# Depthwise convolution in halves of 64 rows, spread over bands 10 to 32, and the projection to 256 over three regions

## Chip, cores and metric

The kernel runs on one core of one Trainium2 chip. The metric is device time in microseconds (us) of one execution; the number given for a kernel is the median of several runs. A run taken with the hardware profiler is a separate execution with its own time, and all durations of single instructions come from it.

The engines are called as in the profile: PE is the tensor engine (PEld its weight loads), ACT the scalar engine, DVE the vector engine, POOL the general engine, SP the engine that issues nearly all DMAs here, one after the other in program order.

## The reference

The kernel computes two layers on x of shape (4, 128, 128, 128): four images, 128 channels, 128 x 128 pixels, all in 32-bit floats. Cut to what matters:

```python
# layer 0
tok  = regions(x, size=16, step=14)              # 9 x 9 regions of 16 x 16 pixels, overlapping by 2
y    = ln(tok) @ w_qkv                           # q, k, v; 4 heads of 32
tok  = softmax(q @ k.T * 32**-0.5) @ v @ w_out + b_out + tok
xf   = average of the overlapping regions, back on the image
y    = ln(xf) @ w_p0 + b_p0                      # 128 -> 256 channels: "the projection to 256"
ym   = depthwise_conv(y, dw_k, 5 x 5, padding 2) # each of 256 channels by itself
ym   = batchnorm(ym)                             # statistics over all images and pixels
x    = gelu(gelu(ym)) @ w_p2 + b_p2 + xf
# layer 1
out  = batchnorm(conv3x3(act_quant(x), weight_quant(w1)))
out  = batchnorm(conv3x3(act_quant(out), weight_quant(w2))) + x
```

The depthwise convolution of an image can begin only as the rows of `y` that it reads are projected, and the GELU stage can begin only when the statistics of the convolution of all four images are there.

## The kernel before

**The bands.** The first stage goes over 36 bands, t = 0 to 35: four images of nine bands, a band being a row of nine regions (`NR` = 9). For each region j the program records one attention: `scores` (PE, then two exponentials of ACT, L792), `halves`, `values_in`, and `values` of the region before. Beside these, `beside(t)` hands out side work to the nine regions as four lists each (`plan`): the layer norm and the q, k projections of band t + 1 (`ln1_chunks`, pieces `a1`, `a2`), the output projection, layer norm and projection to 256 of band t - 1 (`post_chunks`, two chunks `b1` and `b2` of eleven pieces), and steps of the depthwise convolution (`c[j]`, and `d[j]` where a region gets two). The order of the instructions on PE, ACT, DVE and SP is the order in which the program records them (`manual_schedule`); no scheduler moves them. Each engine takes its instructions in that order.

**The projection to 256.** The last four pieces of each chunk, `b1[7:]` and `b2[7:]`, are `p0`: four matmuls of 512 or 384 columns into a PSUM tile `pm` (three buffers), an ACT copy with bias into `y` (L567), and a store of `y` to DRAM (`y2_d`, L431, DMA `y_d<-y`) that is issued by SP after the next piece. There are four `y` tiles, two for each half of the channels, so a fifth `p0` writes where the first one's store must have landed. From band 10 on, the four of `b1` stand in region 8 and the four of `b2` in region 0 of the next band (`left`, `f`). Up to band 9 they are spread over three regions (`full`).

**The depthwise convolution.** `conv_steps(n)` makes the steps of one unit `(b, g, ng)`: image b, `ng` groups of `GR` = 16 rows from group g. A step reads one tile `u` (80 partitions: two half-tiles of 40 rows; `32 * CW` numbers each), does the matmuls of `depthwise` (L601) with a banded weight `w`, has ACT copy two PSUM tiles to `c` (L648), DVE take statistics (L652) and SP store to `cv_d`. With ng = 8 a tile is 4 + 4 channels of eight row groups and a unit has 32 tiles; with ng = 4 it is 8 + 8 channels of four row groups and a unit has 16 tiles. The first step (`begin`) only loads. `load(at + 2)` is issued in step `at`; where a tile begins a new weight block it loads `w` too (L587), just ahead of its four loads of `u` (L634). Pool `up` holds three `u` and three `w`; `c` has two buffers for each of two names.

**When steps run.** `todo` holds the steps, `share[0]` the bands over which they are to be spread. Images 0 and 1 are units of 33 steps over nine bands each (bands 10 to 18 and 19 to 27: 3 or 4 steps a band), image 2 of 33 steps over five (bands 28 to 32: 6 or 7 a band). Image 3 is three units: 17 steps in bands 33 and 34, 17 in band 35, and the rest (`conv_rest`) behind the last band. Before band 10 `todo` holds the preparation of weights.

`st0` keeps the statistics of each unit; `chunk_stats` merges them in `conv_rest`.

Of the kernel before, what the change touches and what calls it, by code (L numbers as in the profile page):

```python
# [8 lines left out]
F32 = mybir.dt.float32  # L9
# [5 lines left out]
P = 128  # L15
# [4 lines left out]
NR = (P - RS) // STEP + 1  # L20
# [11 lines left out]
GR = 16  # L32
CW = P // 2
KD = 2 * (GR + 4)
NCK = 8
# [11 lines left out]
def layers(  # L47
# [29 lines left out]
    nc = tc.nc  # L77
    B = x.shape[0]
# [45 lines left out]
    g1, b1 = vector(ln1_g, "g1"), vector(ln1_b, "b1")  # L124
# [3 lines left out]
    g2, b2 = vector(ln2_g, "g2"), vector(ln2_b, "b2")  # L128
# [7 lines left out]
    with (  # L136
# [21 lines left out]
        for w in (wqkv, wp0.rearrange("p h m -> p (h m)")):  # L158
            n = w.shape[1]
# [7 lines left out]

    bands = [(b, i) for b in range(B) for i in range(NR)]

    units = [(b, 0, P // GR) for b in range(B - 1)] + [(B - 1, g, n) for g, n in ((0, 4), (4, 2), (6, 2))]  # L170

    sctx = ctx.enter_context(ExitStack())
    stp = sctx.enter_context(tc.tile_pool(name=f"st0_{tag}", bufs=1))
# [11 lines left out]
    with ExitStack() as actx:  # L185
        pool = lambda name, bufs, **k: actx.enter_context(
            tc.tile_pool(name=f"{name}_{tag}", bufs=bufs, **k)
        )
# [8 lines left out]
        bctx = actx.enter_context(ExitStack())  # L197
        pool = lambda name, bufs: bctx.enter_context(tc.tile_pool(name=f"{name}_{tag}", bufs=bufs))
        xp, yp, sums = pool("xp", 2), pool("yp", 2), pool("sums", 1)
        up, cp = pool("up", 3), pool("cp", 2)  # L200
        att, attn_t, attn_v = pool("att", 2 if safe else 4), pool("attn_t", 2), pool("attn_v", 2)


# [381 lines left out]
        def weights(wt, k, jj, n, dma):  # L585
            for half in range(2):
                dma(  # L587
                    out=wt[64 * half : 64 * half + KD].rearrange("p s c m -> p s (c m)"),
                    in_=dw_d[2 * k + half, :, :, 256 * jj : 256 * (jj + n)],
                )  # L590
# [24 lines left out]
        def conv_steps(n, ahead=2):  # L615


            b, g0, ng = units[n]
            nc_ = min(8, 32 // ng)
            tiles = [(k, jj, c) for k in range(NCK) for jj in range(2) for c in range(0, 8, nc_)]  # L620
            steps, U, W = [], {}, {}
            nj = nc_ // 4

            def load(at):
                k, jj, c = tiles[at]
                if c == 0:
                    W[k, jj] = up.tile([P, 3, 8, 32], F32, name="w")
                    weights(W[k, jj], k, jj, 1, nc.sync.dma_start)
                ut = up.tile([P, 32 * CW], F32, name="u")[:, : ng * nc_ * CW]
                U[at] = ut = ut.rearrange("p (g c x) -> p g c x", g=ng, c=nc_)  # L630
                for half in range(2):
                    ch = 32 * k + 16 * half + 8 * jj + c
                    for a, z in ((0, GR), (GR, GR + 4)):
                        nc.sync.dma_start(  # L634
                            out=ut[64 * half + 2 * a : 64 * half + 2 * z].rearrange(
                                "p g c x -> p g (c x)"
                            ),
                            in_=input_of(b, g0, ng, ch, nc_, a, z),
                        )

            def products(at):
                k, jj, c0 = tiles[at]
                ut, wt = U.pop(at), W[k, jj]
                pc = [ps_m.tile([P, nj, ng, CW], F32, name="pm") for _ in range(2)]
                depthwise(pc, wt[:, :, c0:], ut, nc_)
                for half in range(2):
                    cv = cp.tile([P, nj, ng, CW], F32, name=f"c{half}")
                    nc.scalar.copy(  # L648
                        cv.rearrange("p j g x -> p (j g x)"), pc[half].rearrange("p j g x -> p (j g x)")
                    )  # L650
                    for j in range(nj):
                        nc.vector.bn_stats(  # L652
                            st0[:, k, half, 2 * jj + c0 // 4 + j, n, :], cv[:, j].rearrange("p g x -> p (g x)")
                        )
                        ch = 32 * k + 16 * half + 8 * jj + c0 + 4 * j
                        store(
                            bass.AP(
                                cv_d[b].tensor,
                                cv_d[b][g0, ch, 0:1].offset,
                                [[CW, P], [2 * P * GR * P, ng], [1, CW]],  # L660
                            ),
                            cv[:, j],
                        )

            def begin():
                for at in range(ahead):
                    load(at)

            steps.append(begin)
            for at in range(len(tiles)):  # L670
                def one(at=at):
                    if at + ahead < len(tiles):
                        load(at + ahead)
                    products(at)

                steps.append(one)
            return steps

        def conv_rest(n, w_t, u_t, c_t):
# [3 lines left out]
            b, g0, ng = units[n]  # L683
            early = 3
            at = GR + 2
# [12 lines left out]
            W = [w_t.tile([P, 3, 16, 32], F32, name=f"w{k}") for k in range(NCK)]  # L698
# [13 lines left out]
            def step(k):  # L712
                sc = ps_s.tile([P, 2, 2, NT], F32, name=f"sc{k % 2}")
                pc = [
                    sc[:, half].rearrange("p a n -> p (a n)").rearrange("p (j g x) -> p j g x", j=4, g=ng)
                    for half in range(2)
                ]
                depthwise(pc, W[k], U[k], 16)
                for half in range(2):
                    cv = c_t.tile([P, 4, ng, CW], F32, name=f"c{half}")  # L720
                    nc.scalar.copy(
                        cv.rearrange("p j g x -> p (j g x)"), pc[half].rearrange("p j g x -> p (j g x)")
                    )
                    for j in range(4):
                        nc.vector.bn_stats(
                            st0[:, k, half, j, n, :], cv[:, j].rearrange("p g x -> p (g x)")
                        )
                    engine = (nc.sync, nc.scalar)[half]
                    for g in range(ng):
                        engine.dma_start(  # L730
                            out=bass.AP(
                                cv_d[b].tensor,
                                cv_d[b][g0 + g, 32 * k + 16 * half, 0:1].offset,
                                [[CW, P], [4 * GR * P, 4], [1, CW]],
                            ),
                            in_=cv[:, :, g],
                        )
# [143 lines left out]
        def beside(t, sel=None):  # L881
# [3 lines left out]
            one = list(early) if t else ln1_chunks(1)  # L885
            early[:] = ln1_chunks(t + 2) if t + 2 < T else []
            two = post_chunks(t - 1, sel) if t else []
            had = len(todo)
            if t >= 2:
                b, i = bands[t - 2]  # L890
                if i == NR - 1 and b < B - 1:
                    todo.extend(conv_steps(b))
                    share[0] = NR if b < B - 2 else 5
                elif b == B - 1 and i == 4:
                    todo.extend(conv_steps(B - 1))
                    share[0] = 2
                elif b == B - 1 and i == 6:
                    todo.extend(conv_steps(B))
                    share[0] = 1

            fresh = len(todo) > had
            n = len(todo) // share[0] if fresh else -(-len(todo) // max(share[0], 1))
            conv = [todo.pop(0) for _ in range(n)]
            share[0] -= 1
            a1, a2 = one if one else ([None] * 9,) * 2
            b1, b2 = two if two else ([None] * 11,) * 2
            if t == T:
# [5 lines left out]

            c = [[] for _ in range(NR)]
            d = [[] for _ in range(NR)]
            twice = len(conv) > NR
            for j in sorted((1, 3, 5, 7, 8, 4, 6, 2, 0)[: len(conv)]):
                c[j] = [conv.pop(0)]
                d[j] = [conv.pop(0)] if twice and j and conv else []
            x1 = lambda: fetch(t, 0)  # L920
            x2 = lambda: fetch(t, 1)
            f, left[:] = list(left), b2[7:]
            s1 = early[0][0] if early else None
            plan = [
                ([a1[1]], [], f, [*c[0], a1[2]]),
                ([], [a1[3], *c[1]], [], [a2[0]]),
                ([a2[1]], [a1[4]], b1[:2], [*c[2], a2[2]]),
                ([], [a2[3], *c[3]], [], [b1[2]]),
                ([b1[3]], [a2[4]], [*a1[5:], *b2[:2]], [*c[4], b1[4]]),
                ([], [b1[5], *c[5]], [], [b2[2]]),  # L930
                ([b2[3]], [b1[6]], a2[5:], [*c[6], b2[4]]),
                ([], [b2[5], x1, *c[7]], [], []),
                ([], [b2[6], x2], b1[7:], [*c[8], s1]),
            ]
            if t == 0:
                plan[0] = ([], [], [], [*c[0], *a1[:3]])
# [12 lines left out]
                    flush(n)  # L949

        T = len(bands)
        todo, share, left, early = [], [0], [], []
        wq, kscale = [], []
        one, two = quantised(0, w1), quantised(1, w2)
        for n in range(len(one) + 1):
            todo += one[n : n + 1] + two[max(n - 1, 0) : n]
        todo += band_matrices()
        share[0] = NR + 1
        for blk in row_blocks(0):
            xb[0, blk[0]] = load_rows(xp, "xt", 0, *blk)  # L960
        bng, bnb = vector(bn_g, "bng"), vector(bn_b, "bnb")
# [445 lines left out]
```

## Time and profile before

| what | us |
|---|---|
| median of 3 runs | 3232.88 (3232.2 to 3239.54) |
| the profiled execution | 3249.98 |
| its span, first to last instruction | 3248.2 |
| bands 0 to 9 (0 to 506.2, with what stands ahead of them) | 506.2 |
| bands 10 to 18 (506.2 to 1022.5) | 516.3 |
| bands 19 to 27 (1022.5 to 1540.2) | 517.7 |
| bands 28 to 32 (1540.2 to 1913.9) | 373.7 |
| bands 33 to 35 (1913.9 to 2195.5) | 281.6 |
| from there to the GELU stage (2322.4) | 126.9 |
| GELU and both 3x3 convolutions (2322.4 to the end) | 925.8 |
| PE busy in the whole span | 3059.6 (94%) |
| ACT, DVE, POOL busy | 1988.5, 2014.5, 840.9 |

A band begins with its first exponential (L792, 18 in a band); the times are read from the trace. In a row of the stretches that are shown below, the numbers are the stretch, its length, the busy time and the instructions of each engine, the granted PE clock as a share of full speed, and the mean busy share of 16 DMA engines with what they moved in GB/s. In a row of the order of time, they are start, length, engine, line, operation, the tiles and shapes, the number of merged instructions and, in brackets, the idle time of the engine ahead of them and what ended it. Every 32-bit matmul of the program stands as two records.

### The profile page before, as it was taken

How to read it: one execution, taken by the hardware profiler on the slowest of the kernel's cores; microseconds unless marked ns; L12 is line 12 of the kernel's file. 1: busy time of each engine (PE TensorE's matmuls, PEld its weight loads, DVE VectorE, ACT ScalarE, POOL GpSimd, SP SyncE). 2: the span in 40 equal slices, each digit the busy share in tenths (PEclk: the TensorE clock that was granted, in tenths of full speed). 3: DMA queues.
4: the chain of work that ended last, by engine and by line, in shares of the span. 5: the costliest groups of instructions: out<-in, count | busy, mean ns of one | idle time of the engine just before them, and what ended most of it. 6: DMA issues, size and time to landing. Idle time of an engine off the chain costs nothing.

```text
span 3248.2 us, 92154 instructions
## 1 busy us (share of the span) xinstructions
PE 3059.6 (94%) x39162; PEld 1480.1 (46%) x39162; DVE 2014.5 (62%) x3244; ACT 1988.5 (61%) x2658; POOL 840.9 (26%) x1058
## 2 busy tenths in 40 slices
PE   7999999999999999999888998876899999999998
PEld 4555544444444444444344444453544444444443
DVE  5777886766766777676555664542455555666543
ACT  5777777777776777677555655432477777433443
POOL 3444443333333333333222232211111111000000
PEclk9999999999999999999999998876799999999999
DMA  3555677888886888886898988857899999452398
GB/s 82 151 167 162 176 186 191 203 199 204 215 193 169 191 206 211 196 213 172 179 202 201 209 188 203 196 158 187 264 354 359 358 359 304 162 167 80 110 357 311
DMA packets 809891, 681.70 MB, mean 210 GB/s; under 512 B 580918, under 2 KB 695935, under 8 KB 809471
## 3 DMA queue, kind: packets, MB, share of 16 engines
q1 hardware_dynamic: 798879, 669.17, 75.8%
q8 instruction: 311, 5.10, 0.7%
q0 software_dynamic: 1024, 3.93, 0.5%
q10 hardware_dynamic: 9568, 2.61, 0.3%
q14 instruction: 109, 0.89, 0.1%
HBM read 408.72 MB, written 270.79 MB: 209 GB/s over the span
## 4 chain that ended last, share of the span: by engine, by line
PE 76%; DMA 9%; ACT 5%; issue 4%; SPq 3%; DVE 2%; ACTq 0%; POOL 0%; DVEq 0%; POOLq 0%
PE pc L1164 21%; PE pm L438 16%; PE sc L784 9%; PE pm L601 9%; PE po L847 8%; PE pb L1228 6%; PE po L855 3%; DMA y_d<-y 3%; PE pm L377 3%; ACT pt L792 2%; DMA u<-y_d 2%; DMA xn<-row 1%; SPq L451 1%; SPq L431 1%; ACT v L775 1%
## 5 line engine op out<-in xcount | busy, mean ns | idle before, releaser
L867 DVE RECIPROCAL rd<-po 128x256 f32<-128x256 f32 x324 | 568.8, 1756 | 439.1 <-PE po L855 438.5
L1164 PE MATMUL pc<-q,wq 128*128 128x512 fp8e4 x3168 | 700.3, 381 | 5.1 <-DVE q L1176 5.1
L792 ACT ACTIVATE pt<-sc 128x1024 f32<-128x1024 f32 x648 | 628.2, 1025 | 119.1 <-PE sc L784 63.2
L802 POOL TENSOR_TENSOR sm<-pt 128x512 f32<-128x512 f32 x324 | 415.7, 1283 | 1047.3 <-ACT pt L792 727.0
L1164 PEld LDWEIGHTS <-wq 128*128 128x128 fp8e4 x3168 | 309.0, 98 | 406.7 <-issue 38.9
L784 PE MATMUL sc<-q,kr 32*128 32x256 f32 x5184 | 413.6, 417 | 27.3 <-ACT pt L792 27.1
L601 PE MATMUL pm<-u,w 40*32 40x504 f32 (+5 forms) x7680 | 369.6, 503 | 41.7 <-DMA u<-y_d 29.7
L784 PEld LDWEIGHTS sc<-q,kr 32*128 32x128 f32 x5184 | 254.1, 191 | 286.4 <-issue 177.1
L847 PE MATMUL po<-pt,v 128*32 128x256 f32 x5184 | 364.9, 401 | 10.0 <-DVE part L871 6.9
L648 ACT COPY c<-pm 128x512 f32<-128x512 f32 (+1 forms) x256 | 132.4, 563 | 272.3 <-PE pm L601 243.3
L438 PE MATMUL pm<-xn,wp 128*32 128x512 f32 (+1 forms) x2304 | 248.1, 553 | 44.6 <-ACT y L567 42.6
L567 ACT ACTIVATE y<-pm,vectors 128x512 f32<-128x512 f32 (+1 forms) x288 | 183.1, 641 | 166.0 <-DMA y_d<-y 111.9
L802 DVE TENSOR_TENSOR sm<-pt 128x512 f32<-128x512 f32 x324 | 244.2, 754 | 35.8 <-ACT pt L792 35.8
L438 PE MATMUL pm<-xn,wqkv 128*32 128x512 f32 (+1 forms) x2304 | 245.3, 548 | 4.9 <-ACT v L775 3.5
L601 PEld LDWEIGHTS pm<-u,w 40*32 40x32 f32 x7680 | 147.6, 112 | 223.1 <-issue 153.0
L652 DVE BATCH_NORM_STATS2 st<-c 128x6 f32<-128x512 f32 (+2 forms) x320 | 160.9, 550 | 134.8 <-ACT c L648 134.3
L1228 PE MATMUL pb<-cv,wp 128*128 128x512 f32 x512 | 232.1, 596 | 4.9 <-ACT cv L1219 4.9
L847 PEld LDWEIGHTS po<-pt,v 128*32 128x32 f32 x5184 | 140.5, 112 | 186.5 <-issue 103.5
L1172 DVE BATCH_NORM_STATS2 st<-pc 128x6 f32<-128x512 f32 x256 | 165.7, 689 | 84.7 <-PE pc L1164 84.7
L855 PE MATMUL po<-sm,ones 128*32 128x256 f32 x2592 | 206.1, 389 | 0.0
L874 POOL TENSOR_TENSOR ob<-ob,part 128x32 f32<-128x32 f32 x288 | 127.2, 442 | 230.6 <-DVE part L871 224.8
L438 PE MATMUL pm<-wqkv,yr 128*32 128x128 f32 x5184 | 176.3, 273 | 1.2 <-issue 1.2
(157 smaller groups left out, 3394.2 us busy)
## 6 DMA issues: line engine op xcount, KB each, us to landing
cv<-cv_d SPq DMA_DIRECT2D x64, 1024.0 KB
u<-y_d SPq DMA_DIRECT2D x234, 256.0 KB
cv_d<-c SPq DMA_DIRECT2D x192, 256.0 KB
y_d<-y SPq DMA_DIRECT2D x160, 256.0 KB
xn<-row SPq DMA_DIRECT2D x76, 512.0 KB
xfl<-xf_d SPq DMA_DIRECT2D x64, 512.0 KB
id_d<-y SPq DMA_DIRECT2D x64, 512.0 KB
idt<-id_d SPq DMA_DIRECT2D x64, 512.0 KB
```

Of the source, the lines that this page charges most:

```text
L438: nc.tensor.matmul(out[m], w[:, m], v, start=True, stop=True)
L567: nc.scalar.activation(y[:, :n], pm[:, : n * P].rearrange("p (r c e) -> p r e c", r=n, e=2), AF.Identity, bias=bp0[:, h : h + 1],)
L601: nc.tensor.matmul(outs[half][32 * q : 32 * q + 32, j, :, a:z], wt[hs, s, c, :], ut[hs, :, c, a + s - 1 : z + s - 1], start=(s == 1), stop ...
L784: nc.tensor.matmul(sc[h // 2][:, h % 2, kc, :].rearrange("p (r c) -> p r c", c=RS), region(kr, j)[hs, kc * P : (kc + 1) * P], queries(j, h ...
L792: nc.scalar.activation(pt, sc[p], AF.Exp)
L802: add(sm, pt[:, :, 0, :], pt[:, :, 1, :], ALU.add)
L847: nc.tensor.matmul(po[hs, 0, :], v[:, kc, hs], pt[h // 2][:, h % 2, kc, :], start=(kc == 0), stop=(kc == 1),)
L855: nc.tensor.matmul(po[hs, 1, :], ones, sm[h // 2][:, h % 2, :], start=True, stop=True)
L867: nc.vector.reciprocal(rd, po[:, 1, :])
L1164: nc.tensor.matmul(pc[:, h], w[:, t, :], q1[b][:, r + dy : r + dy + RB, dx : dx + P], start=(t == 0), stop=(t == 8),)
L1172: nc.vector.bn_stats(st[:, 2 * n + h, :], pc[:, h])
L1228: nc.tensor.matmul(pb[:, m], wp2[:, h, :], cv[:, h, px], start=(h == 0), stop=(h == 1))
```

## The change

Four things change.

1. Images 0 to 2 are cut into two units of 64 rows each (ng = 4) instead of one of 128 (ng = 8). The steps per image go from 33 to 34; a step keeps its size, but has 48 matmuls of 256 columns where it had 24 of 512, four stores of 128 KB where it had two of 256 KB, and its own weight block where two steps shared one.
2. The 102 steps of images 0 to 2 are given out evenly over the bands 10 to 32 (`left_over`): five a band in bands 10 to 19, four in bands 20 to 32. A unit joins when its rows are there (`waiting`). Bands 33 to 35 keep their numbers of steps.
3. The weights of a step are loaded one step ahead (`load_weights(at + 1)`), into a pool `wp` of two buffers. `c` has one name with three buffers, in `conv_rest` too.
4. From band 10 to 31 the last two `p0` of `b1` move from region 8 to the next band: two in region 8, three in region 0, three in region 2 (`f[:3]`, `f[3:]`). Band 32 and later keep four and four.

```diff
-    units = [(b, 0, P // GR) for b in range(B - 1)] + [(B - 1, g, n) for g, n in ((0, 4), (4, 2), (6, 2))]
+    units = [(b, g, 4) for b in range(B - 1) for g in (0, 4)] + [(B - 1, g, n) for g, n in ((0, 4), (4, 2), (6, 2))]
...
-        up, cp = pool("up", 3), pool("cp", 2)
+        up, wp, cp = pool("up", 3), pool("wp", 2), pool("cp", 3)
...
+            def load_weights(at):
+                if at == len(tiles):
+                    return
+                k, jj, c = tiles[at]
+                if c == 0:
+                    W[k, jj] = wp.tile([P, 3, 8, 32], F32, name="w")
+                    weights(W[k, jj], k, jj, 1, nc.sync.dma_start)
+
             def load(at):
                 k, jj, c = tiles[at]
-                if c == 0:
-                    W[k, jj] = up.tile([P, 3, 8, 32], F32, name="w")
-                    weights(W[k, jj], k, jj, 1, nc.sync.dma_start)
...
-                    cv = cp.tile([P, nj, ng, CW], F32, name=f"c{half}")
+                    cv = cp.tile([P, nj, ng, CW], F32, name="c")
...
             def begin():
+                load_weights(0)
                 for at in range(ahead):
                     load(at)
...
                 def one(at=at):
+                    load_weights(at + 1)
                     if at + ahead < len(tiles):
                         load(at + ahead)
                     products(at)
...
-                    cv = c_t.tile([P, 4, ng, CW], F32, name=f"c{half}")
+                    cv = c_t.tile([P, 4, ng, CW], F32, name="c", bufs=3)
...
-                if i == NR - 1 and b < B - 1:
-                    todo.extend(conv_steps(b))
-                    share[0] = NR if b < B - 2 else 5
...
-            n = len(todo) // share[0] if fresh else -(-len(todo) // max(share[0], 1))
+                if i in ((4, 6) if b == B - 1 else (4, NR - 1)):
+                    waiting.append(conv_steps(2 * b + (i > 4)))
+            last = T - NR + 6
+            while t > NR and waiting:
+                todo.extend(waiting.pop(0))
+            if t <= NR:
+                n = -(-len(todo) // (NR + 1 - t))
+            elif t < last:
+                n = min(len(todo), -(-left_over[0] // (last - t)))
+                left_over[0] -= n
+            else:
+                n = len(todo) // 2 if t == last else len(todo)
...
-                d[j] = [conv.pop(0)] if twice and j and conv else []
+                d[j] = [conv.pop(0)] if j and len(conv) > NR - 1 - j else []
...
-            f, left[:] = list(left), b2[7:]
+            apart = t + 1 < last
+            f, left[:] = list(left), [*(b1[9:] if apart else []), *b2[7:]]
+            g = 3 if t < last else len(f)
...
-                ([a1[1]], [], f, [*c[0], a1[2]]),
+                ([a1[1]], [], f[:g], [*c[0], a1[2]]),
...
-                ([a2[1]], [a1[4]], b1[:2], [*c[2], a2[2]]),
+                ([a2[1]], [a1[4]], [*f[g:], *b1[:2]], [*c[2], a2[2]]),
...
-                ([], [b2[6], x2], b1[7:], [*c[8], s1]),
+                ([], [b2[6], x2], b1[7 : 9 if apart else None], [*c[8], s1]),
...
+        left_over = [2 * (B - 1) * (2 * NCK + 1)]
```

## The prediction

> **What bounds the kernel now.** I read the chain of work that ended last, to see which engine sets the time; then the busy time by stretches with a cut at every band; then the order of time on PE, ACT and SP where the slow bands lose theirs.
>
> ```profile
> PE 76%; DMA 9%; ACT 5%; issue 4%; SPq 3%; DVE 2%; ACTq 0%; POOL 0%; DVEq 0%; POOLq 0%
> ```
>
> PE sets the time, and DMA waits are next. The bands, by stretches (band 10; 19; 20; then 28 to 35):
>
> ```profile
> 506.20:566.00 59.80, 56.12 (x848) 26.90 (x840) 38.95 (x61) 41.35 (x62) 19.66 (x25) 0.97 0.84 193
> ...
> 1022.50:1082.70 60.20, 57.11 (x832) 27.14 (x824) 37.50 (x59) 40.30 (x60) 19.59 (x25) 0.94 0.82 183
> 1082.70:1138.80 56.10, 55.98 (x928) 26.56 (x923) 40.32 (x63) 41.48 (x65) 21.14 (x27) 1.00 0.84 189
> ...
> 1540.20:1608.60 68.40, 65.01 (x984) 29.71 (x976) 40.54 (x65) 43.47 (x67) 19.90 (x25) 0.95 0.80 173
> 1608.60:1688.00 79.40, 71.21 (x1072) 32.43 (x1068) 45.38 (x71) 44.74 (x71) 21.12 (x27) 0.94 0.92 201
> 1688.00:1763.30 75.30, 68.63 (x1072) 31.91 (x1068) 43.98 (x69) 44.61 (x70) 21.13 (x27) 0.95 0.90 205
> 1763.30:1843.10 79.80, 71.05 (x1072) 32.07 (x1068) 45.32 (x70) 44.71 (x70) 21.13 (x27) 0.94 0.89 202
> 1843.10:1913.90 70.80, 65.71 (x1024) 29.89 (x1020) 43.20 (x68) 43.59 (x68) 21.13 (x27) 0.95 0.89 201
> 1913.90:1996.50 82.60, 75.24 (x1397) 41.37 (x1390) 43.36 (x79) 44.92 (x70) 21.11 (x27) 0.90 0.83 192
> 1996.50:2094.80 98.30, 83.84 (x1592) 45.68 (x1591) 49.68 (x95) 46.19 (x73) 19.98 (x24) 0.86 0.83 198
> 2094.80:2195.50 100.70, 74.99 (x1908) 48.37 (x1909) 40.58 (x100) 35.23 (x62) 15.38 (x18) 0.78 0.63 167
> ```
>
> Band 20, with four products, is all PE at full clock. Bands 29 to 31, with seven, lose 4 to 9 us of idle PE and run at a clock of 0.94 to 0.95. What one product costs PE, with 512 columns and with 256:
>
> ```profile
> 655.66 2.78 PE L601 MATMUL pm<-u,w 40*32 40x512 f32 x48
> ...
> 1943.99 2.79 PE L601 MATMUL pm<-u,w 40*32 40x256 f32 x96
> ```
>
> So a band without products is 56.10 - 4 x 2.78 = 45.0 us, and band 29 should take 45.0 + 7 x 2.78 = 64.5; it takes 79.4. Its successor shows where that goes (first PE, then ACT, then SP, as band 30 begins):
>
> ```profile
> 1690.07 2.39 PE L438 MATMUL pm<-xn,wp 128*32 128x384 f32 x24
> 1696.94 0.98 PE L438 MATMUL pm<-xn,wp 128*32 128x384 f32 x8 [4.48 <-ACT y L567]
> ```
> ```profile
> 1696.30 0.58 ACT L567 ACTIVATE y<-pm,vectors 128x384 f32<-128x384 f32 x1 [5.40 <-DMA y_d<-y]
> ```
> ```profile
> 1688.14 3.49 SPq L451 DMA_DIRECT2D xr<-in_x_dram  x1
> 1691.72 3.56 SPq L431 DMA_DIRECT2D y_d<-y  x3
> ```
>
> The fifth `p0` needs the `y` tile of the first; that tile's store was issued some 9 us after the copy, because SP first had the loads and stores of the step in region 7 and a fetch of `xr`. ACT stands, the three `pm` fill, PE stands, and the clock is granted at half for 3.4 us at a time after it (eight such windows, two of them doubled, between 1608 and 1865). In bands 28 to 32 the excess over 45.0 + 2.78 per product is 9.5, 14.9, 10.8, 15.3 and 9.1 us: 60 together. Bands 10 and 19 (two products, floor 50.6) lose 9.2 and 9.6, to the same wait and to the first loads of an image, which must wait for its last `y`. The four-product bands 11 to 16 and 20 to 25 take 57.4 in the mean, 1.3 above 56.1.
>
> **The change, part by part.**
>
> *Halves of 64 rows.* PE: 96 products of 2.79 us instead of 96 of 2.78: 1 us. ACT: two copies of 128x512 a step as before. DVE: four statistics of 413 ns (the 128x256 row) for two of 684: 0.28 us a step, beside a DVE at 40 of 57 us; without that cover it would be 27 us. The Trainium skill ("TensorE: Matmul & The Clock Gate", on the 56 ns gap) speaks against small matmuls: about 62 ns each when the sequencer decodes them in software, by which 96 records would take 6 us and the change would cost some 300 us. The row above has 96 in 2.79, 29 ns each, so the measurement decides, and the sum goes by it.
>
> *More issues on SP.* A step issues four `u`, two `w`, four stores: 10, where it was seven on average. By medians (`u` 0.35, `w` 0.77, store 0.46 us) that is 4.8 us against 3.1. A five-step band has 18 + 50 = 68 issues: 24 us for the steps, 8 for the rest and the waits in the queue (SP now holds 30 to 34 us in a four-step band), some 45 of 60. It hides while SP is not the bound; that is the second rival. DMA time: shares of 0.85, 0.90 and 0.87 in bands 11 to 13 are 49.6 us of all engines in the mean, 0.92, 0.90 and 0.89 in bands 29 to 31 are 70.6, so 7.0 a step. The second weight block adds 120 packets of 1 KB at 79 ns over 16 engines, 0.6, and the longer `u` packets give back 0.2 (640 of 79 ns against 320 of 147, the means of the packet records by size). A five-step band then wants 58.6 us, a four-step band 51.2. The skill ("DMA: Bandwidth & Descriptors", how many engines) has a copy of 40 partitions run on ten engines only, so the weights would load those more than the mean shows; no trace here tells the engines apart.
>
> *Even spread and three regions.* Between a `p0` and the one that needs its tile there is as much PE work as before, but only one `p0` of region 0 now depends on a store of region 8, where four did, and PE has `scores` and `values` (1.15 + 1.68 us) to run while ACT stands. Four-step bands have no step in region 8 at all. I take the stall of a four-step band at 1.0 us (1.3 now; from 0.3 to 2). A five-step band shows nowhere: at least nothing over its floor (band 20 has that), 1 us as the low end; at most what a DMA share of 0.92, the highest in any band, allows: 58.6 / 0.92 = 63.7, 5.6 over the floor. I take 3, as the step in region 8 keeps part of the late store. First loads of an image no longer wait, since they read rows done bands ago.
>
> Bands 10 to 19: 10 x 45.0 + 47 products x 2.79 + 5 (two bands with 16 rows instead of 14, 2.3 to 2.7 each) = 586, + 30 = 616; before 576.5. Bands 20 to 32: 13 x 45.0 + 49 x 2.79 + 5 = 727, + 13 = 740; before 831.2. Together 1356 against 1407.7: **52 saved**.
>
> *Weights one step ahead, three `c`.* In bands 10 to 32 steps lie 11 to 19 us apart, and a weight issued where SP now loads `u` would land with 2 us or more to spare; only region 7 to 8 (9 us) is tight. In bands 33 to 35 it isn't spare: putting each weight where the next step's was issued, with 2.3 us to land (as their packets show there), 21 of 28 steps find it 0.2 to 7.0 us late, 65 us added up. SP is behind PE there, so a stall that PE pays lets SP catch up, and the next is smaller. Low end 2 us gained (the first step of a unit waits for one weight less), high end 35, half of it paid; I take 12. A copy of ACT into the third `c` waits for the store of the step before instead of two before; 16 of 32 would come 1 to 8 us before that store is even issued, hidden partly by the same stalls: 2 more. The longer merge of statistics (54 numbers for 36) adds 0.7 behind the last step. **14 to 15 lost.**
>
> Sum: 1356 - 1407.7 + 14 = -38 on a span of 3248.2: 3210. The profiled execution lies 17 above the median, so 3232.9 - 38 = **3195 us**.
>
> **The rivals.**
>
> *Late weights take it all back (slower, 0.14).* If lag isn't caught up, bands 33 to 35 pay the 65 us, and region 8 of each five-step band pays what the nearest rows of band 28 lack (3.5 us late) with half a clock window of 3.4, 5.2 x 10 = 52: 3195 + 51 + 52 = 3298. It turns slower when 38 us of that is paid, a third. For it: those bands already stand at a clock of 0.78 to 0.90. Against: own slack of weights there is 1 to 16 us now, and each stall slows the copies that SP waits for.
>
> *SP or DMA bounds the five-step bands (0.14).* At 0.92 they take 63.7, or about 5.6 over the floor: 3195 + 26 = 3221. For it: shares of 0.92 in band 29. Against: band 34 passes 107 issues in 98.3 us, 0.92 each, and 68 at that are 62.6.
>
> *The waits vanish wholly (0.12).* 1 and 0.3 of stall, nothing in the tail: 587 + 9 + 727 + 4 = 1327, 81 saved: 3152.
>
> That the steps don't land as said is excluded: the built order has the matmuls of five and four steps in those bands and `p0` as 3, 3 and 2.
>
> **How the numbers follow.** The forecast has 0.60. Runs spread by 0.23%, so 0.3% (9.7 us) is told from nothing. Faster takes most of the forecast (0.57), the third rival (0.12) and some of the second (0.05): 0.74. Same is the rest of the second and a forecast with a dear tail: 0.11. Slower is the first and a little of the second: 0.15. The range goes from the low ends (3152 less a little) to the high ends together, 63.7 and 2 us a band and 35 in the tail: 642 + 753 - 1407.7 + 35 = +22, 3255; I cut it to 3150 to 3250.
>
> **What would show it.** Bands 28 to 32 at 56 to 58 us with a clock near 1.00 and hardly any ACT wait for `y_d<-y`; bands 10 to 19 near 61.6; 96 records in 2.79 us. Wrong: five-step bands over 65.4 us (from there on the gain is gone), DMA waits of L601 for `w` in region 8, or bands 33 to 35 with what follows longer than 408.5 by more than 35.

## The result, and the profile after

The changed kernel takes 3325.56 us in the median of four runs (3312.16 to 3334.82), the kernel before 3236.21 (3232.2 to 3243.94, four runs): a ratio of 1.027, with an interval of 1.0227 to 1.0313. It is slower by 89 us where 38 saved were forecast. The profiled executions stand alike: 3322 against 3250 us, spans 3320.0 and 3248.2. The chain of waits and the group of the convolution's matmuls, from the page of the changed kernel, and the same group from the page of the kernel before:

```profile
PE 74%; DMA 12%; ACT 5%; issue 4%; DVE 3%; SPq 2%; POOL 0%; ACTq 0%; DVEq 0%; POOLq 0%
...
L601 PE MATMUL pm<-u,w 40*32 40x252 f32 (+3 forms) x12288 | 400.1, 389 | 82.1 <-DMA w<-dw_d 42.9
```
```profile
L601 PE MATMUL pm<-u,w 40*32 40x504 f32 (+5 forms) x7680 | 369.6, 503 | 41.7 <-DMA u<-y_d 29.7
```

DMA on the chain went from 9% of 3248 to 12% of 3320, some 110 us more; ahead of the matmuls of the convolution PE now stands 82 us, 43 of it until a weight has landed (before, 41.7, most of it for `u`). By stretches (bands 10, 17, 19, then 20, 29, 32, then 33 to 35; the columns are those of the stretches shown before):

```profile
505.30:572.50 67.20, 61.03 (x1140) 32.44 (x1128) 42.05 (x74) 42.00 (x65) 19.68 (x25) 1.00 0.80 192
973.70:1048.90 75.20, 66.17 (x1204) 34.75 (x1200) 42.94 (x76) 43.05 (x66) 21.96 (x27) 0.92 0.84 203
1123.80:1195.40 71.60, 68.71 (x1240) 35.92 (x1240) 42.29 (x76) 43.35 (x65) 19.62 (x25) 0.91 0.80 190
1195.40:1249.70 54.30, 53.13 (x1000) 28.77 (x1000) 39.36 (x67) 40.27 (x63) 21.15 (x27) 1.00 0.79 201
1738.70:1801.70 63.00, 58.51 (x1119) 31.70 (x1112) 41.31 (x72) 41.33 (x65) 21.12 (x27) 0.95 0.85 196
1920.80:1979.80 59.00, 58.42 (x1136) 31.38 (x1128) 41.47 (x72) 42.53 (x66) 21.11 (x27) 1.00 0.81 203
1979.80:2071.30 91.50, 76.77 (x1400) 42.05 (x1396) 45.98 (x83) 44.98 (x70) 21.16 (x27) 0.89 0.82 189
2071.30:2162.30 91.00, 80.35 (x1596) 44.62 (x1596) 47.69 (x90) 46.06 (x73) 19.88 (x24) 0.92 0.82 194
2162.30:2267.70 105.40, 76.85 (x1909) 49.05 (x1905) 40.65 (x99) 35.73 (x62) 15.35 (x18) 0.73 0.60 162
```

Bands 10, 13 and 16 have five steps but four products, because the first step of a unit only loads; the seven bands with five products take 68.5 to 75.3 us, where 61.6 was forecast for the mean of bands 10 to 19, at a clock of 0.91 to 0.92 where PE stood long. Bands 20 to 32 take 54.3 to 63.0, not 57. The DMA share is not higher than before but lower: 0.81 over bands 10 to 32, where it was 0.84 and 0.86. By stages, in us of the profiled executions:

| stage | before | forecast | after |
|---|---|---|---|
| bands 10 to 19 | 576.5 | 616 | 690.1 |
| bands 20 to 32 | 831.2 | 740 | 784.4 |
| bands 33 to 35 | 281.7 | | 287.9 |
| from there to the end | 1052.6 | | 1052.3 |
| the last two rows together | 1334.3 | +14 | 1340.2 |

Band 17 shows how a five-step band loses its time. First one piece of the chain (its start, its length, what it is), then SP, PE and ACT in order of time:

```profile
1032.29 7.95 DMA w<-dw_d
```
```profile
1031.28 0.36 SPq L411 DMA_DIRECT2D xn<-row  x1
1031.68 0.51 SPq L451 DMA_DIRECT2D xr<-in_x_dram  x1
1032.29 2.54 SPq L587 DMA_DIRECT2D w<-dw_d  x2
1034.87 1.59 SPq L639 DMA_DIRECT2D u<-y_d  x4
1036.57 5.18 SPq L431 DMA_DIRECT2D cv_d<-c  x4
```
```profile
1040.37 6.42 PE L601 MATMUL pm<-u,w 40*32 40x256 f32 x96 [5.52 <-DMA w<-dw_d]
```
```profile
1046.07 0.59 ACT L653 COPY c<-pm 128x512 f32<-128x512 f32 x1 [10.30 <-PE pm L601]
```

The weight was issued from 1032.3 on and could be used at 1040.2, 8 us later. Read from the packets of 1 KB, which in this kernel are the weights', the two loads of a block take 6.0 us from the first issue to the last packet in the median of bands 10 to 32, and 4.2 in bands 33 to 35 of the kernel before. PE stands 5.5 us; the product then takes 6.42 us instead of 2.79, at a granted clock of 0.50; ACT stands 10.3 us before it can copy, and the next stores of `c` wait for that. The product itself is as cheap as forecast where the clock is full, as in band 22:

```profile
1319.44 2.79 PE L601 MATMUL pm<-u,w 40*32 40x256 f32 x96
```

In the four-step bands it is still `y`. The waits of ACT and PE in bands 10 to 32 (waiting, waited for, us in total, times, longest):

```profile
ACT y L567 <- DMA y_d<-y: 39.3, 10, 6.4
PE pm L601 <- DMA w<-dw_d: 23.8, 18, 5.5
ACT c L653 <- DMA cv_d<-c: 14.4, 10, 2.6
```

All 18 waits for weights lie in bands 10 to 19, all of the 39 us for `y` in bands 20 to 32.

### The profile page after: what moved, and what is told of

It is laid out like the page before. It is cut to its first block, busy times and chain, and to the rows that moved or that the text cites. A ratio compares the mean times of both kernels' runs of the same rounds, so it can differ in the third digit from the quotient of the medians.

```text
span 3320.0 us, 101883 instructions
## 1 busy us (share of the span) xinstructions
PE 3105.1 (94%) x43770; PEld 1596.2 (48%) x43770; DVE 2035.6 (61%) x3436; ACT 1987.2 (60%) x2658; POOL 840.5 (25%) x1058
## 4 chain that ended last, share of the span: by engine, by line
PE 74%; DMA 12%; ACT 5%; issue 4%; DVE 3%; SPq 2%; POOL 0%; ACTq 0%; DVEq 0%; POOLq 0%
PE pc L1170 21%; PE pm L438 15%; PE pm L601 9%; PE sc L791 8%; PE po L854 8%; PE pb L1234 6%; DMA w<-dw_d 4%; PE po L862 3%; PE pm L377 3%; DMA cv_d<-c 2%; DMA y_d<-y 2%; ACT pt L799 2%; DVE rd L874 1%; DMA u<-y_d 1%; DMA row<-rstd 1%
## 5 line engine op out<-in xcount | busy, mean ns | idle before, releaser
L601 PE MATMUL pm<-u,w 40*32 40x252 f32 (+3 forms) x12288 | 400.1, 389 | 82.1 <-DMA w<-dw_d 42.9
L601 PEld LDWEIGHTS pm<-u,w 40*32 40x32 f32 x12288 | 256.5, 113 | 223.9 <-issue 99.3
L657 DVE BATCH_NORM_STATS2 st<-c 128x6 f32<-128x256 f32 (+1 forms) x512 | 175.2, 398 | 222.4 <-ACT c L653 221.6
```

What stands on the lines that cost most here:

```text
L601: nc.tensor.matmul(outs[half][32 * q : 32 * q + 32, j, :, a:z], wt[hs, s, c, :], ut[hs, :, c, a + s - 1 : z + s - 1], start=(s == 1), stop ...
L657: nc.vector.bn_stats(st0[:, k, half, 2 * jj + c0 // 4 + j, n, :], cv[:, j].rearrange("p g x -> p (g x)"))
```

## The experiments

Sixteen more kernels ran. Each ratio is to runs of the kernel before on the same chip; differences in us are differences of ratios times 3236. "Stages" are bands 10 to 19, 20 to 32 and 33 to 35 of the profiled execution, one for each kernel.

| run | what it is | ratio, interval | stages, us |
|---|---|---|---|
| before | | 1 | 576.5, 831.2, 281.7 |
| after | the change | 1.027 (1.0227 to 1.0313) | 690.1, 784.4, 287.9 |
| w2 | weights two steps ahead | 1.0232 (1.0187 to 1.0277) | 681.1, 794.3, 280.9 |
| w2c4 | and four `c` | 1.0272 (1.0221 to 1.0322) | |
| oldspread | old numbers of steps | 1.025 (1.0217 to 1.0283) | 590.1, 890.1, 287.3 |
| wskip | half of the weight blocks | 0.9974 (0.9948 to 1.0) | 641.4, 761.2, 264.3 |
| wtiny | those, but issued and tiny | 1.002 (1.0 to 1.0039) | 658.4, 753.3, 276.1 |
| wskip_old | wskip, old numbers of steps | 0.9982 (0.9963 to 1.0001) | 565.3, 847.4, 266.1 |
| wpool | weights on POOL's queue | 1.0045 (1.0025 to 1.0065) | 656.9, 785.5, 258.2 |
| wact | weights on ACT's queue | 1.014 (1.0103 to 1.0177) | 677.3, 766.3, 286.3 |
| w48 | 48 rows in a weight load | 1.0279 (1.0242 to 1.0315) | 701.4, 789.1, 287.5 |
| yact | `y` on ACT's queue | 1.0103 (1.0073 to 1.0133) | 658.5, 750.6, 292.1 |
| y10w | wpool, and `y` on ACT from band 10 | 1.0007 (0.998 to 1.0033) | 653.5, 765.0, 262.6 |
| wown | before + a block for each step | 1.0134 (1.0115 to 1.0152) | 592.7, 857.3, 284.5 |
| three | before + three regions | 0.9958 (0.9941 to 0.9974) | 567.1, 823.3, 277.9 |
| three_y10w | three + as in y10w | 0.9915 (0.9898 to 0.9932) | 578.0, 824.7, 263.5 |
| three_late | the same, late bands alone | 0.9848 (0.9829 to 0.9866) | 567.2, 822.4, 261.8 |
| three_late48 | and 48 rows | 0.9897 (0.9876 to 0.9917) | 569.9, 815.6, 258.8 |

### Are the weights late, or `c` short? (w2, w2c4)

```diff
+                load_weights(1)
-                    load_weights(at + 1)
+                    load_weights(at + 2)
-        up, wp, cp = pool("up", 3), pool("wp", 2), pool("cp", 3)
+        up, wp, cp = pool("up", 3), pool("wp", 3), pool("cp", 3)
```

For room, the statistics of units 6 to 8 are written over those of units 0 to 2. w2c4 also has two buffers for each of two names of `c`, as before.

> The changed kernel with weights loaded two steps ahead into three buffers, as far ahead as before the change; to make room, the statistics of units 6 to 8 overwrite those of units 0 to 2. Theory L (late weights: a step in region 8 needs its weights 9 us after they can be issued and they take 7 to 8 us): DMA waits of L601 for w fall from 24 us in bands 10 to 19 to under 5, the half-clock windows behind them go, bands 10 to 19 fall from 690 us to 640 or less, the median from 3326 to 3280 or less. Theory Q (the SP queue and the DMA engines are too full with ten issues a step, whatever is issued first): the same transfers wait as long, bands 10 to 19 stay over 675, the median within 15 us of 3326.

> As the kernel with weights two steps ahead, and c again with two buffers for each of two names. Theory L says that c matters little in bands 10 to 32 (14 us of ACT waits for cv_d in bands 10 to 19): 0 to 15 us below that kernel. If three c buffers were a main cause, over 30 us below it.

Two steps ahead, PE doesn't wait for a weight once in bands 10 to 32, and 12 us are gained, inside the intervals; bands 10 to 32 take as long as in the changed kernel (1475.4 us for 1474.5). The waits went elsewhere (w2, bands 10 to 32):

```profile
ACT c L653 <- DMA cv_d<-c: 56.0, 21, 6.6
ACT y L567 <- DMA y_d<-y: 41.0, 10, 8.1
...
PE pm L377 <- ACT sq L371: 33.2, 11, 5.6
```

24 us for weights became 42 more for stores of `c`, and 30 more in which PE waits for ACT. A fourth `c` gained nothing either: in bands 10 to 32 ACT's waits for stores of `c` fall from 56 to 0.2 us, and those for `y` rise from 41 to 89. A missing buffer or a late order is not the cause; something makes whatever lands last late.

### Is it the spread? (oldspread)

```diff
-                n = min(len(todo), -(-left_over[0] // (last - t)))
-                left_over[0] -= n
+                n = ((3, 4, 4, 4, 4, 4, 4, 4, 3) * 2 + (7, 7, 7, 7, 6))[t - NR - 1]
```

> The changed kernel, but its steps given out as before the change: 34 over nine bands, 34 over nine, 34 over five. Theory H (a step of half the rows costs more by itself, through ten issues on SP instead of seven and its own weights, so a denser band costs more): bands 28 to 32 with seven steps take 400 us or more, where they took 374, bands 10 to 27 take 1060 or more, where they took 1034, and the median is 3280 or more. Theory S (the halves are harmless, five steps in each of ten bands are the fault): bands 10 to 27 within 10 us of 1034, bands 28 to 32 within 10 of 374, the median 3225 to 3255.

No: with the old numbers of steps the halves are as slow. Bands 28 to 32 take 418 us where whole images took 374.

### Is it the weights? (wskip, wtiny, wown, wpool)

```diff
                 k, jj, c = tiles[at]
+                if jj:
+                    W[k, jj] = W[k, 0]
-                if c == 0:
+                elif c == 0:
```

> The changed kernel with weights loaded for every second tile only, as often as before the change; the other tiles use the weights of the tile before them. If the doubled weight loads are the main cost (by their bytes, their place in the queue, or by being late): bands 10 to 19 fall from 690 us to 640 or less, the median from 3326 to 3270 or less. If it is the stores of 128 KB, or the five steps as such: within 20 us of 3326.

Without the second block of each pair the changed kernel is 96 us faster, more than all it had lost. But 64 blocks are left out: the 48 that the change added in images 0 to 2, and 16 of image 3 that the kernel before loads too. In bands 10 to 32, where only the 48 count, the profiled execution is 72 us shorter than the changed kernel's (1402.6 for 1474.5) and 5 shorter than that of the kernel before (1407.7). And it takes away issues on SP, bytes, and waits at once. wtiny keeps the issues:

```diff
                 if jj:
                     W[k, jj] = W[k, 0]
+                    bit = wp.tile([P, 3, 8], F32, name="bit")
+                    for half in range(2):
+                        nc.sync.dma_start(
+                            out=bit[64 * half : 64 * half + KD],
+                            in_=dw_d[2 * k + half, :, :, 256 * jj : 256 * jj + 8],
+                        )
```

> The changed kernel, but the second weight block of each pair of steps is only touched: the same two loads are issued by SP at the same places, of the same 120 pieces but 32 bytes each instead of 1 KB, into a tile that no product reads; the products use the block of the step before. (Half of the weights are left out, as in the run that loaded every second block; its output differs.) Theory A, the places in SP's queue cost: the loads behind them in order are as late as in the changed kernel, so the time stays above 3290 us, bands 10 to 19 above 670. Theory B, the 240 KB a step cost DMA time (or the products wait for them to land): the time is that of the run without the second block, 3215 to 3245, bands 10 to 19 at 635 to 650. Between 3245 and 3290 both have a share, split by where it lies. I lean to A with 0.5, to B with 0.25.

I had leaned to the issues and was wrong. The tiny loads cost SP as much as the full ones (wtiny, SP in order of time):

```profile
1001.38 1.57 SPq L632 DMA_DIRECT2D bit<-dw_d  x2
1013.07 1.57 SPq L587 DMA_DIRECT2D w<-dw_d  x2
```

and still 81 of the 96 us are gained, 63 of the 72 in bands 10 to 32 (1411.7 us). The issues at their places are worth the remaining 15 (the two intervals touch), the bytes and the wait for them 81; w2 lays at most some 12 of that on the wait, and none of it in bands 10 to 32.

> The kernel before, whole images of 128 rows and its own spread, but each step of images 0 to 2 loads its own weight block where two steps shared one: 48 more blocks, 96 more issues on SP, two steps ahead as before. Theory A (the second weight block makes the halves slow, whichever way): the same 48 blocks whose removal from the changed kernel gave 96 us are added here, so +40 to +95 us, 3275 to 3330; most of it in bands 28 to 32, where SP and the transfers are fullest (374 to over 400). Theory B (it costs only beside the four stores of a half and the weights one step ahead): under +20 us, 3235 to 3255. Theory C (it is harmless and the halves cost by their 96 small matmuls): within 8 us.

The converse, on the kernel before:

```diff
-                if c == 0:
-                    W[k, jj] = up.tile([P, 3, 8, 32], F32, name="w")
+                if c == 0 or ng == 8:
+                    W[at] = W[k, jj] = up.tile([P, 3, 8, 32], F32, name="w")
```

The same 48 blocks, two steps ahead and with whole images, cost 43 us, at the low end of what was expected. They are no wait for weights there: ACT's waits for `y_d<-y` in bands 10 to 32 grow from 76 to 107 us (the kernel before, then wown):

```profile
ACT y L567 <- DMA y_d<-y: 76.3, 58, 7.2
```
```profile
ACT y L567 <- DMA y_d<-y: 107.4, 64, 7.4
```

Whether their bytes or their issues do it in this kernel was not separated.

> The changed kernel with the weights of a step issued by POOL, on a queue of its own; the same bytes. If the SP queue is what is full (1.6 us of issue a step, and whatever waits ahead of them there): bands 10 to 19 at 645 us or less, the median at 3275 or less. If the DMA engines are what is full, or the time from issue to landing counts: bands 10 to 19 over 670, the median over 3300.

`weights(..., nc.gpsimd.dma_start)` alone gains 73 us: the same bytes, but not between the `u`, `c` and `y` of SP's queue. It moves all 128 blocks, those of image 3 too: by the profiled executions 33 us are gained in bands 10 to 19, none in bands 20 to 32 (785.5 for 784.4), and 30 in bands 33 to 35, whose weights the kernel before loads on SP as well.

### Why less on another queue? (wact, w48)

> The changed kernel with the steps' weights issued by ACT instead of SP: another queue, but pieces of 1 KB as on SP's, where POOL's queue moved them as pieces of 4 KB. Theory Q (the weights must only be out of SP's queue, where u, c and y stand behind them): most of POOL's 75 us is found here too, less what two issues of 0.77 us a step cost an ACT that is busy 42 of 60 us: 3240 to 3285. Theory P (POOL's larger pieces made the gain): it stays at 3300 or more, and the products wait for w as before. I lean to Q, 0.65.

Weights issued by ACT (`nc.scalar.dma_start`) gain 42 us, between what the two theories expected. No product in bands 10 to 32 waits for `w`, and the four-step bands take 766 us, 18 less than in the changed kernel. But bands 10 to 19 gain 13 only (waits there):

```profile
ACT c L653 <- DMA cv_d<-c: 60.3, 22, 7.3
```

So packets of 1 KB gain too once they have left SP's queue, and POOL's pieces of 4 KB aren't needed for it; but how much of POOL's 73 us is the queue, how much the issues that SP no longer makes and how much the pieces isn't settled.

```diff
+                rows = KD + 8 if 2 * k + half < 2 * NCK - 1 and n == 1 else KD
```

> The changed kernel, its weight blocks loaded with 48 rows for each half instead of 40 (the eight more are rows of the next block, which no product reads; the very last block keeps 40): a fifth more bytes, the same issues at the same places. Theory L (each byte of weights in SP's queue costs, wherever it runs): 23 MB become 28, so 0 to 20 us slower, a ratio to the kernel before of 1.026 or more. Theory K (the 40 rows load a part of the 16 engines only, and those are behind while the mean stands at 0.81): faster by 20 to 65 us, a ratio of 1.007 to 1.021, bands 10 to 19 under 680. The trace is what speaks for K so far: at most 8 to 15 packets of 1 KB overlap while a pair of weight loads runs, where loads of 128 rows reach 17 to 20. The Trainium skill (DMA: Bandwidth & Descriptors, section on why a DMA increments its semaphore by 16, how many engines) has the same: the largest number up to 16 that divides the rows, 10 for 40 and 16 for 48, and for SP and ACT always the lowest-numbered. I give K 0.6.

Theory K fell. With 48 rows the packets of a pair do spread: by the packet records 10 to 22 of them overlap where 8 to 15 did, as the Trainium skill ("DMA: Bandwidth & Descriptors", the section on why a DMA increments its semaphore by 16) would have it for 16 engines in place of ten. The two loads of a block also land sooner, 5.0 us after the first issue for 6.0 (medians of bands 20 to 32), and SP needs 0.60 us to issue one for 0.77. The time doesn't move: 1.0279 for 1.027, with a fifth more bytes. That speaks against few engines as the cost, but doesn't exclude that the added bytes took back a gain.

### Stores of `y` elsewhere (yact, y10w)

> The changed kernel with the stores of y issued by ACT right behind the copy, not by SP. If a store of y is late because it stands in the SP queue behind loads and waits: ACT waits for y_d in bands 20 to 32 fall from 39 us to under 10, those bands from 784 to 755, the median to 3290 or less (also fewer issues on SP). If it is late because it lies in the DMA rings behind 1 MB of loads: the waits stay over 25 us and the median within 15 us of 3326.

With `y` issued by ACT right behind its copy the changed kernel gains 54 us, although bands 0 to 9 lose 28 (533 for 505), where nothing had been late. The four-step bands take 57.7 us instead of 60.3, near the 56.9 that the prediction had for them, so the late store of `y` was most of their loss. Bands 10 to 19 gain about as much (32 us of 690). Bands 10 to 32 together take 1409.1 us, so 65 of the 67 us that the change had lost there are back with every weight still on SP's queue, where moving the weights gave back 31 (wact) and 32 (wpool).

> As the kernel with the weights on POOL, and the stores of y issued by ACT from band 10 on. If both lengthen the time by standing in the SP queue, the gains add: bands 20 to 32 at 750 us as with the stores of y on ACT, bands 10 to 19 at 630 or less, bands 0 to 9 as before (506), the median at 3230 or less. If the DMA engines are full, it is no better than the kernel with the stores of y on ACT throughout less what that lost in bands 0 to 9 (28 us): 3250 or more.

With weights on POOL and `y` on ACT from band 10 on, the changed kernel comes level with the kernel before, not below it.

### What is the even spread worth? (wskip_old)

> Every second weight block left out, as in the run at 3229.7, but with 3 or 4 steps a band in bands 10 to 27 and 6 or 7 in 28 to 32, as before the change; half of the weights are left out. It shows what the even spread itself is worth once the weights don't stand in the way. Theory E (the spread brings what the prediction said, some 50 us): 3270 or more, bands 28 to 32 at 375 or more and bands 10 to 27 at 1025 or more. Theory N (beyond four steps a band each further step costs 5.5 to 6.5 us wherever it stands, so that the spread moves the cost and saves none): 3215 to 3245. I lean to N, 0.55.

Nothing that can be measured: 0.9982 with the old numbers of steps, 0.9974 with the even ones, both with half of the weights. Bands 20 to 32, then band 28 to 32 alone, of the one with the old numbers, and bands 28 to 32 of the even one:

```profile
1072.80:1920.20 847.40, 803.28 (x15445) 436.12 (x15440) 552.94 (x965) 551.68 (x843) 272.02 (x346) 0.97 0.83 198
1536.30:1920.20 383.90, 347.71 (x6744) 190.20 (x6737) 222.98 (x404) 222.14 (x343) 104.06 (x133) 0.94 0.85 196
```
```profile
1614.60:1908.00 293.40, 287.72 (x5488) 155.62 (x5482) 205.46 (x352) 207.27 (x317) 104.10 (x133) 0.98 0.82 197
```

Bands 28 to 32 do gain 90 us, as meant, and bands 10 to 27 lose 80 (1028.8 to 1109.2). In the even run a five-step band takes 64.1 us and a four-step band 58.6: the fifth step costs 5.6. In the other, 76.8 for 6.8 steps against 57.2 for 3.8 make 6.5 each. So a step beyond the fourth costs 5.6 to 6.5 us in both spreads, twice its 2.79 us of PE.

### On the kernel before, and a faster kernel (three, three_y10w, three_late, three_late48)

```diff
-            f, left[:] = list(left), b2[7:]
+            apart = NR < t < T - 4 and (t + 1) % NR != 1
+            f, left[:] = list(left), [*(b1[9:] if apart else []), *b2[7:]]
+            g = 3 if t < T - 3 and t % NR != 1 else len(f)
```

> The kernel before with the projection over three regions alone (bands 11 to 31 but not across the first band of an image, whose loads read those rows). If spreading takes the waits for y away, as the prediction had it: bands 28 to 32 fall from 374 to 345 or less and the median from 3236 to 3205 or less. If only the distance between a y and its store counts, which the order leaves as it was: 3226 to 3246, with ACT waits for y_d of 35 us or more in bands 28 to 32.

The third part of the change alone helps, by 0.4%: bands 10 to 27 lose their small waits, bands 28 to 32 gain 6 us.

> The kernel before with the projection spread over three regions, with the stores of y issued by ACT from band 10 on, and the weights of the steps issued by POOL: what helped each kernel, without the halves. If SP's queue is what makes y late, bands 28 to 32 fall from 368 to 340 or less, and the whole to 3185 to 3205, 0.985 to 0.991 of the kernel before. If the transfers themselves are the bound there (16 engines busy 0.9 of the time), bands 28 to 32 stay at 360 or more and the whole at 3215 to 3235.

The second of the two: bands 28 to 32 stay at 363, the whole at 3222 us. What is gained over three regions alone lies in bands 33 to 35 (263.5 for 277.9), while bands 10 to 19 lose 11.

> The kernel before with the projection over three regions; y stored by ACT only from band 28 on, and weights issued by POOL only for the images 2 and 3. The version with both from band 10 on gained 18 us in bands 28 to 35 and lost 17 in bands 10 to 27 against three regions alone. If that loss is ACT's and POOL's issues in bands where nothing was late, it is not paid here: bands 10 to 27 at 1020 to 1026, the whole 0.982 to 0.989 of the kernel before. If the two traces differed by chance of one execution, 0.989 to 0.996.

```diff
+                    if t >= 3 * NR:
+                        nc.scalar.dma_start(out=dst, in_=src)
...
+weights(W[k, jj], k, jj, 1, nc.gpsimd.dma_start if b >= 2 else nc.sync.dma_start)
```

The fastest kernel of the study, ahead of both: 3203.02 us, 0.9848 (0.9829 to 0.9866). Bands 10 to 27 took 1028.8 us, not the 1020 to 1026 expected, yet less than the 1039.6 of three_y10w.

> The kernel before with three regions, late y on ACT and late weights on POOL (0.985 of the kernel before), and 48 rows in each load of the steps' weights. Theory K: 33 steps of two images and the last image's share a block for two steps or more, so a third of what it brings in the changed kernel: 0.978 to 0.985. Theory L: 0.985 to 0.988.

No gain: 0.9897, measured on another chip than the 0.9848, so that this family is 1.0 to 1.5% ahead of the kernel before.

These runs also settle a reading of the prediction. ACT's waits for the stores of `y` in bands 28 to 32, first in the kernel before, then in three, then in three_late, and last that stretch of three_late:

```profile
ACT y L567 <- DMA y_d<-y: 45.2, 16, 7.2
```
```profile
ACT y L567 <- DMA y_d<-y: 18.5, 4, 7.6
```
```profile
ACT y L567 <- DMA y_d<-y: 3.0, 2, 1.9
```
```profile
1534.70:1895.50 360.80, 340.37 (x5184) 150.92 (x5180) 219.68 (x339) 221.82 (x340) 124.12 (x165) 0.96 0.90 205
```

42 us of waiting for `y` are gone, 13 us of time. The DMA share rose from 0.88 to 0.90 only.

## Why the prediction was wrong

**Two steps failed.** The first is "More issues on SP", which put the added weight loads at nothing: "It hides while SP is not the bound", with 0.6 us of DMA a step, 1.2 for each of the 48 blocks, as transfers that nothing waits for. Its cover was the slack of SP (45 of 60 us), and SP did have it: its issues fill 784 us of bands 10 to 32 in the changed kernel and 785 with the tiny loads, which give back 63 us there. What wasn't covered were the transfers. The 48 blocks cost 1.3 us each in bands 10 to 32 of the changed kernel (62.8 / 48; with those of image 3, 81 / 64, the same) and 0.9 in the kernel before (43 / 48).

Of the loss against the forecast, 110 us by the two spans (72 lost for 38 saved), 74 lie in bands 10 to 19 and 44 in bands 20 to 32; the rest of the kernel did better by 8. Of the 118 in bands 10 to 32, 72 go when the second blocks do (wskip), 63 of them with the bytes alone (wtiny). The other 47 (1402.6 for 1356) are the second failed step.

**"Even spread and three regions: 52 saved"**, the second, was wrong by itself. It took bands 28 to 32's 60 us of excess as late stores of `y` that would go with the seven steps. The wait can be taken away (45.2 to 3.0 us) and 13 us come back. The excess goes with the steps, at 5.6 to 6.5 us for each beyond four, and the spread moves them to bands that then pay the same. The numbers of the prediction could have warned: 58.6 us of DMA in a five-step band of 61.6 is a share of 0.95, above the 0.92 that it had itself named the highest of any band. The stall of 3 was taken below the price that its own rival gave (63.7). Without the weights' loss such a band took 64.1 us. No run shows more than 0.90 over the whole of bands 10 to 19, 20 to 32 or 28 to 32, which would fit a limit of the transfers near there; but single bands of other runs reach 0.95 (wpool, band 25) and 0.97 (y10w, band 14), and bands 10 to 19 of wskip stand at 0.85, so what a step beyond the fourth waits for is not shown.

**"Stall of a four-step band 1.0 us"**: 4.4 measured ((784.4 - 727) / 13), most of it for `y`: with `y` on ACT a band takes 57.7, 1.8 over the floor. The mechanism named (one `p0` instead of four depending on region 8) does help, as three shows; with ten issues a step ahead of it, the store of `y` was late again.

**The five-step stall of 3** was 10.4 ((690.1 - 586) / 10).

**"Weights one step ahead, three `c`": 14 lost** was of the right sign; with all behind band 32 it was 5.9 (1340.2 - 1334.3), in one execution of each kernel.

**Right were** 2.79 us for 96 small matmuls, and with them the floor, and the sign of trouble that was named: waits of L601 for `w`, five-step bands over 65.4 us.

**The rivals.** "Late weights" had the right side and the wrong mechanism: it laid 51 us in bands 33 to 35, which paid 6, and 52 on lateness in bands 10 to 19, which still take 681.1 us for 690.1 when no product waits for a weight (w2). That it came near the measured 3325 with 3298 is luck. "SP or DMA bounds the five-step bands" had the right part of the kernel, but priced it at 26 us, by a DMA share of 0.92 where 0.81 was measured. "The waits vanish wholly" is out.

**What stays open.** How a block in SP's queue turns into 0.9 to 1.3 us. Its 240 packets of 59 ns are 0.9 us over 16 engines, but these are busy only 0.81 of bands 10 to 32. wtiny excludes the issues alone, w2 the wait for the weights, and w48 speaks against their few engines. What is left, that stores of `c` and `y` behind them come late, agrees with wpool, wact and yact and with the waits that moved in w2 and wown. They leave SP later rather than travel longer: where ACT waited for a store of `y` in bands 20 to 32, that store was issued 4.5 us behind its copy in the kernel before, 7.0 in wown, 6.6 in the changed kernel and 4.3 with the tiny loads, and it landed 4.9, 4.5, 4.0 and 4.1 us after that (medians of 37, 37, 10 and 9 waits, read from the order of copies and stores in the traces). A candidate for why is that SP stands ahead of a store (L431) until a weight that it had issued before has landed; the changed kernel, bands 10 to 19, then 20 to 32:

```profile
SPq L431 <- DMA w<-dw_d: 39.2, 52, 2.8
```
```profile
SPq L431 <- DMA w<-dw_d: 38.6, 59, 2.6
```

With the tiny loads the two are 16.4 and 27.5 us. But in wown this wait doesn't grow (13.6 us in bands 20 to 32, 18.5 in the kernel before), so it isn't the whole, and no run tested it.

## What to carry to other kernels

A load that hides behind no wait today still takes its place among the transfers: when a change adds transfers to a queue that others depend on, price them at what they move, and test them with tiny copies at the same places, which tell the bytes from the issues. Count which transfers a test takes away: here 16 of 64 blocks were not the change's, and the stages told them apart. An excess that the profile lays on one wait isn't that wait's price: here 42 us of waiting were removed for 13 us of time. Before spreading work evenly, divide the transfer time of the forecast by its length; if the share is above any that the profile shows, the forecast needs a reason why it should be reached.

## What the runs showed of the hardware

A load of 32-byte pieces cost SP as long to issue as one of 1 KB pieces: 1.57 us for two loads of 120 pieces each, both. The same weights went over POOL's queue as pieces of 4 KB (5760 more packets of that size in bands 10 to 32, where SP's were 23040 of 1 KB), and POOL needed 1.35 us for the two. The Trainium skill ("DMA: Bandwidth & Descriptors", the section that issuing engines are not separate DMA queues) says that issuing from several engines saves only the time of issuing. Here leaving out the issues of 64 blocks was worth 15 us (wskip against wtiny), moving all 128 blocks to ACT gained 42 and to POOL 73; whether that is more than SP's issues, no run here separates.
